# A graph attention layer on one core: the softmax sums one turn behind the scores, one-hots made first, four row buffers

## The chip, the cores and the metric

One Trainium2 chip, and of it one core: TensorE (PE), VectorE (DVE), ScalarE (ACT), GpSimd (POOL) and the queue engine SyncE (SP). The metric is the device time of one execution in microseconds; lower is better.

## The reference

There are 12,500 nodes with 128 features and 400,000 edges, sorted by target. Two blocks follow each other, each with a layer norm, a ReLU, a graph layer and a residual. The first graph layer is relational: two rounds that average rows by relation and multiply them with ten matrices. The second is graph attention (GAT), with four heads of 32 features, and the change lies in it:

```python
xl = (x @ W_l).reshape(n, H, C)
xr = (x @ W_r).reshape(n, H, C)
xj = xl[src]
xi = xr[dst]
e = jax.nn.leaky_relu(xi + xj, NEG_SLOPE)
score = jnp.einsum('ehc,hc->eh', e, att)
m = jax.ops.segment_max(score, dst, num_segments=n)
ex = jnp.exp(score - m[dst])
denom = jax.ops.segment_sum(ex, dst, num_segments=n)
alpha = ex / (denom[dst] + 1e-16)
out = jax.ops.segment_sum(alpha[..., None] * xj, dst, num_segments=n)
return out.reshape(n, H * C) + bias
```

A softmax over the edges of each target needs the largest score of a target before its exponentials, and a target's edges can lie across two groups of edges.

## The kernel before

The edges are cut into G = 125 groups of 128 x 25 edges: each of 128 partitions holds J = 25 consecutive edges of the sorted list. A first stage (up to about 450 us) makes tables, a second (to about 4400 us) and a third (to about 8340 us) do the two relational rounds, and the fourth, from about 8370 us to the end, does the attention. Each edge stage fetches a group's source rows by 25 indirect DMAs that GpSimd issues, one for each of the 25 edge columns (`gather`, L365; `gather_halves`, L382, in the stages before). A row in the attention stage has 132 numbers: `xl` and its four products with the attention vector.

In the attention stage the order of the instructions on each engine is the order in which they are written, since a manual schedule is in force (L893): a loop over turns `t` (L894), and in each turn steps that belong to different groups. In turn t:

- `gather` and `load` (L897, L898) for group t. `load` fetches by SP's queue the first target's number, the target rows `xr`, rows of targets `db` and the penalties `pen`.
- `prepare` (L932) for group t: VectorE makes `st` (L779) and `mk` (L782), ACT makes `pk`, and four matmuls make `xn` (L788), the target rows of each partition's first and last edges in its two halves.
- scores for group t-1, in four parts of 7, 6, 7 and 5 edge columns (`PARTS`). For each, ACT copies the first target's row into `z`, a PSUM tile (`first_xr`, L794), and VectorE replaces it where the target changes (L800), adds the gathered rows (L802), multiplies (L804) and reduces (L806). Two `z` copies for the first two parts stand at the turn's start, the others behind parts 0 and 1.
- `maxima` for group t-1: running maxima along each partition in both directions (scans, L760 and L763), transposed by TensorE and copied by ACT to `ro`.
- `inflow` for group t-3: two scans over the 128 partitions (`tr`, L830, and `br`, L835 and L839) carry maxima from one partition to the next. `tr` begins with the last value of the group before, copied by ACT (L829). `br` begins with eight partitions of the group after, so its `ro` must be there. TensorE transposes both and ACT copies them to `io` (L845).
- `less_maxima` for group t-3: L851 takes `io` in, scans spread the maxima, and they are subtracted from the scores (L857).
- `sums` for group t-3: five times for five columns, ACT makes exponentials (L862), VectorE weights the rows with them (`xw`, L863) and makes one-hots of the targets (`s`, L867), and TensorE adds up five matmuls (L871). `xw` and `s` have three buffers each. A last matmul (L874) takes in the group before.
- for group t-4: ACT copies the sums from PSUM to `su` (L906), and `finish` divides by the denominators (L880 to L883), adds the residual (L885) and stores the rows (L887). The last two groups go to a scratch table as well, and the last 128 rows of the output are copied from it at the end (L937).

Gathered rows have five buffers (`gx`, L731), and they are needed from turn t to turn t+3.

Of the kernel before, what the change touches and what calls it, by code (L numbers as in the profile page):

```python
# [9 lines left out]
F32 = mybir.dt.float32  # L10
# [3 lines left out]
OP = mybir.AluOpType  # L14
# [4 lines left out]
P = 128  # L19
J = 25  # L20
# [6 lines left out]
def kernel(  # L27
# [29 lines left out]
    nc = tc.nc  # L57
# [243 lines left out]
    def sorted_edges():  # L301
# [4 lines left out]
        with tc.tile_pool(name="sd", bufs=1, space=DRAM) as sd, tc.tile_pool(name="sk", bufs=1) as sk:  # L306
# [66 lines left out]
            with tc.tile_pool(name="mid", bufs=1) as mid:  # L373
# [58 lines left out]
                def sums(ps, s, rs, rows):  # L432

                    for k in range(2):
                        for c in range(2):
                            a, b = s[:, 2 * k + c, :], rs[k][:, c, :]
                            if not rows:
                                a, b = b, a
                            nc.tensor.matmul(ps, a, b, start=(k == 0 and c == 0), stop=(k == 1 and c == 1),  # L439
                                             skip_group_check=True)  # L440
# [287 lines left out]


            PARTS = [(j0 + a, min(JP, n - a), k) for k, (j0, n) in enumerate(HALVES) for a in range(0, n, JP)]  # L730
            with tc.tile_pool(name="gk", bufs=1) as kp, tc.tile_pool(name="gx", bufs=5) as xp, \  # L731
                    tc.tile_pool(name="gw", bufs=2) as wp, tc.tile_pool(name="gs", bufs=3) as sp, \
                    tc.tile_pool(name="gc", bufs=4) as cp, tc.tile_pool(name="gn", bufs=6) as np_, \
                    tc.tile_pool(name="gp", bufs=1, space=PSUM) as p1, \
                    tc.tile_pool(name="gp2", bufs=2, space=PSUM) as p2:
# [55 lines left out]
                def first_xr(xn, part):  # L791
                    j0, n, k = part
                    z = p2.tile([P, JP, D], F32, name="z")
                    nc.scalar.copy(z[:, :n, :], xn[:, 2 * k, None, :].to_broadcast([P, n, D]))  # L794
                    return z
# [30 lines left out]
                def inflow(g, ros, pens, before):  # L826

                    tr = wp.tile([H, P + 1], F32, name="tr")
                    nc.scalar.copy(tr[:, 0:1], before[:, P:] if g else lows)  # L829
                    nc.vector.tensor_tensor_scan(tr[:, 1:], pens[g][:, 0, :], ros[g][:, 0, :], tr[:, 0:1],  # L830
                                                 op0=OP.add, op1=OP.max)
                    br = wp.tile([H, P + 8], F32, name="br")
                    if g < G - 1:

                        nc.vector.tensor_tensor_scan(br[:, P + 7:P - 1:-1], pens[g + 1][:, 1, 7::-1],  # L835
                                                     ros[g + 1][:, 1, 7::-1], LOW, op0=OP.add, op1=OP.max)
                    else:
                        nc.scalar.copy(br[:, P:P + 1], lows)
                    nc.vector.tensor_tensor_scan(br[:, P - 1::-1], pens[g][:, 1, ::-1], ros[g][:, 1, ::-1],  # L839
                                                 br[:, P:P + 1], op0=OP.add, op1=OP.max)  # L840
                    pc = p1.tile([P, 2 * P], F32, name="px")[:, :2 * H].rearrange("p (k h) -> p k h", k=2)
                    nc.tensor.transpose(pc[:, 0, :], tr[:, :P], ident[:H, :H])
                    nc.tensor.transpose(pc[:, 1, :], br[:, 1:P + 1], ident[:H, :H])
                    io = wp.tile([P, 2, H], F32, name="io")
                    nc.scalar.copy(io, pc)  # L845
                    return io, tr

                def less_maxima(g, sc, sm, io, pk):

                    for k, (e, j) in enumerate(ends):  # L850
                        nc.vector.scalar_tensor_tensor(sm[:, :, j], io[:, k, :], e[:, g:g + 1], sm[:, :, j],  # L851
                                                       op0=OP.add, op1=OP.max)
                    up = wp.tile([P, H, J], F32, name="up")
                    scan_up(up, pk, sm)
                    mx = wp.tile([P, H, J], F32, name="dn")
                    scan_down(mx, pk, up)
                    nc.vector.tensor_sub(sc, sc, mx)  # L857

                def sums(g, xs, sc, po, before):
                    for j0 in range(0, J, JW):  # L860
                        xw = sp.tile([P, JW, H, AW], F32, name="xw")
                        nc.scalar.activation(xw[:, :, :, C], sc[:, :, j0:j0 + JW].rearrange("p h j -> p j h"), AF.Exp)  # L862
                        nc.vector.tensor_mul(  # L863
                            xw[:, :, :, :C], xs[:, j0:j0 + JW, :D].rearrange("p j (h c) -> p j h c", h=H),
                            xw[:, :, :, C:].to_broadcast([P, JW, H, C]))
                        s = sp.tile([P, JW, P], F32, name="s")
                        nc.vector.tensor_tensor(s, iotab[:, None, :].to_broadcast([P, JW, P]),  # L867
                                                dst_b[:, g, j0:j0 + JW, None].to_broadcast([P, JW, P]),
                                                op=OP.is_equal)
                        for j in range(JW):  # L870
                            nc.tensor.matmul(po, s[:, j, :], xw[:, j].rearrange("p h a -> p (h a)"),  # L871
                                             start=(j0 + j == 0), stop=(j0 + j == J - 1), skip_group_check=True)
                    if g:
                        nc.tensor.matmul(po[0:1, :], ecol[:, g - 1:g], before, start=False, stop=True,  # L874
                                         skip_group_check=True)
# [12 lines left out]
                    if g >= G - 2:  # L888
                        nc.sync.dma_start(o_d[ds(b, P), :], o)

                xs, xn, xr, dbs, bs, pens, scs, sms, ros, pks, x2s, pos, sums_of = ({} for _ in range(13))
                tr = None
                with tc.manual_schedule():  # L893
                    for t in range(G + 4):  # L894

                        if t < G:
                            xs[t] = gather(xp, xl_d[:N, :], src_i[:, t, :], XW)  # L897
                            xr[t], dbs[t], pens[t], bs[t] = load(t)  # L898
                        q = t - 3
                        if 0 <= q < G:  # L900
                            x2s[q] = cp.tile([P, D], F32, name="x2")
                            nc.sync.dma_start(x2s[q], x2_d[q])
                        q = t - 4
                        if 0 <= q < G:
                            sums_of[q] = cp.tile([P, H * AW], F32, name="su")
                            nc.scalar.copy(sums_of[q], pos.pop(q))  # L906
                        q = t - 1
                        if 0 <= q < G:
                            scs[q] = cp.tile([P, H, J], F32, name="sc")
                            zs = [first_xr(xn[q][0], p) for p in PARTS[:2]]  # L910
                        q = t - 3
                        if 0 <= q < G:
                            io, tr = inflow(q, ros, pens, tr)
                        q = t - 1
                        if 0 <= q < G:
                            for i, p in enumerate(PARTS[:2]):
                                scores(zs[i], xs[q], *xn[q][:2], scs[q], p)
                                zs.append(first_xr(xn[q][0], PARTS[2 + i]))
                        q = t - 4
                        if 0 <= q < G:  # L920
                            finish(q, sums_of[q], x2s.pop(q), bs.pop(q))
                        q = t - 3
                        if 0 <= q < G:
                            less_maxima(q, scs[q], sms.pop(q), io, pks.pop(q))
                        q = t - 1
                        if 0 <= q < G:
                            for i, p in enumerate(PARTS[2:]):
                                scores(zs[2 + i], xs[q], *xn[q][:2], scs[q], p)
                            pks[q] = xn.pop(q)[2]
                            sms[q], ros[q] = maxima(xs[q], scs[q], pks[q])  # L930
                        if t < G:
                            xn[t] = prepare(t, xr.pop(t), dbs.pop(t))  # L932
                        q = t - 3
                        if 0 <= q < G:
                            pos[q] = p1.tile([P, H * AW], F32, name="po")
                            sums(q, xs.pop(q), scs.pop(q), pos[q], sums_of.pop(q - 1, None))
                nc.sync.dma_start(out[N - P:N, :], o_d[N - P:N, :])  # L937


# [423 lines left out]
```

## Time and profile before

| | |
|---|---|
| median of 3 runs (range) | 12567.6 us (12566.2 to 12571.2) |
| the profiled execution, its span | 12565.0 us, 12563.2 us |
| first and last gather of the attention stage | 8370.8, 12479.3 us |
| busy from 8370.8 to the last gather's end at 12480.2 (4109.4 us) | DVE 3433.6, POOL 3157.4, PE 1322.0, ACT 655.7 us |
| from the last gather's end to the span's end | 83.0 us |
| a gather | 0.944 us at its shortest, 1.010 in the mean, 0.30 between two |
| L863 and L867 | 0.82 us each, five of each for a group |
| busy over the whole span | DVE 73%, POOL 73%, PE 26%, ACT 20% |

Times in views of the profile are in us from the span's start. A group of instructions is shown as line, engine, operation, tiles, count, then busy time and the mean ns of one, then the engine's idle time just before these instructions and what ended most of it. A row of the timeline has start, duration, engine, line, operation and tiles; idle time before it, if any, stands in brackets. "issue" means that nothing shown was waited for.

### The profile page before, as it was taken

To read this page: it belongs to the slowest core of one execution; us is meant where nothing else is said; L and a number is where in the kernel's file an instruction comes from. 1 tells how busy PE (TensorE), PEld (TensorE's weight loads), DVE (VectorE), ACT (ScalarE), POOL (GpSimd) and SP (SyncE) were. 2 spreads that over 40 slices of the span, in tenths; PEclk is the share of its full clock that TensorE was granted. 3 is DMA by queue.
4 is the path that set the end of the run, shared out by engine and by line. 5 is a ranking of instruction groups with operands and counts; after the bars stand their busy time and mean duration, and the time that the engine had idled before them with its cause. 6 is when DMAs were issued, how large, how long until landed. Compare 5 with 4: busy or idle time off the path is not lost.

```text
span 12563.2 us, 69544 instructions
## 1 busy us (share of the span) xinstructions
PE 3260.9 (26%) x12778; PEld 2155.0 (17%) x12778; DVE 9221.3 (73%) x12886; ACT 2511.7 (20%) x6895; POOL 9143.9 (73%) x9384
## 2 busy tenths in 40 slices
PE   7422222222222211111111111113333333333333
PEld 3111111111111100000000000012222222232323
DVE  5777777777777666666666666668888888888888
ACT  3333333333333300000000000001111111111111
POOL 0477777777777777777777777767777777777775
PEclk9655555555555555555555555556666666666666
DMA  6433333333333222222222222222222222222222
GB/s 211 139 94 95 96 96 96 96 95 94 97 96 96 86 62 61 61 61 61 61 61 61 61 61 61 61 59 62 62 61 62 62 63 61 62 61 63 61 63 47
DMA packets 608616, 964.64 MB, mean 77 GB/s; under 512 B 193888, under 2 KB 413610, under 8 KB 608170
## 3 DMA queue, kind: packets, MB, share of 16 engines
q0 software_dynamic: 300000, 621.40, 20.5%
q1 hardware_dynamic: 278906, 267.68, 6.6%
q10 hardware_dynamic: 29264, 71.04, 1.5%
q14 instruction: 340, 2.79, 0.1%
q8 instruction: 106, 1.74, 0.1%
HBM read 758.60 MB, written 200.85 MB: 76 GB/s over the span
## 4 chain that ended last, share of the span: by engine, by line
POOL 62%; issue 24%; DVE 5%; DMA 5%; PE 3%; ACT 1%; ACTq 0%; DVEq 0%; SPq 0%; POOLq 0%
POOL xs L382 43%; POOL xs L365 20%; DMA xs<-t_d,idx 3%; PE ps L288 2%; PE po L871 1%; DMA xs<-xl_d,src_i 1%; DVE z L802 1%; DVE z L800 1%; DVE lr L804 1%; DVE sc L806 1%; DMA xt<-in_x_dram 0%; ACT z L794 0%; DVE s L867 0%; PE pa L294 0%; DVE up L760 0%
## 5 line engine op out<-in xcount | busy, mean ns | idle before, releaser
L382 POOL DMA_INDIRECT xs<-t_d,idx x6250 | 5984.6, 958 | 1941.3 <-issue 1862.7
L365 POOL DMA_INDIRECT xs<-xl_d,src_i x3125 | 3157.4, 1010 | 984.4 <-issue 931.3
L402 DVE TENSOR_TENSOR y<-xs,wk 128x3072 f32<-128x3072 f32 (+1 forms) x375 | 1324.6, 3532 | 1229.5 <-DMA xs<-t_d,idx 1215.0
L405 DVE TENSOR_REDUCE r<-y 128x256 f32<-128x3072 f32 (+1 forms) x375 | 2102.2, 5606 | 30.5 <-DVE y L402 0.9
L414 ACT ACTIVATE y<-xs,wk 128x128 f32<-128x128 f32 x3000 | 1202.6, 500 | 639.6 <-DMA xs<-t_d,idx 616.8
L439 PE MATMUL ps<-r,s 128*128 128x128 f32 x1000 | 305.5, 461 | 3390.8 <-DVE r L405 3390.8
L592 PE MATMUL pt<-wall,hT 128*128 128x512 f32 x750 | 639.2, 989 | 1533.4 <-ACT ts L594 1533.4
L871 PE MATMUL po<-xw,s 128*128 128x132 f32 x6250 | 933.2, 317 | 70.0 <-DVE s L867 60.7
L871 PEld LDWEIGHTS po<-xw,s 128*128 128x128 f32 x6250 | 896.4, 228 | 118.9 <-issue 116.8
L439 PEld LDWEIGHTS ps<-r,s 128*128 128x128 f32 x1000 | 231.9, 322 | 3517.8 <-DVE r L405 3517.8
L121 ACT ACTIVATE sd<-mv,epsc 128x1 f32<-128x1 f32 x223 | 63.6, 293 | 3549.4 <-DVE mv L119 3524.4
L820 PE MATMUL px<-ident,up 128*4 128x128 f32 x125 | 46.5, 372 | 2398.1 <-DVE up L760 2398.1
L596 DVE TENSOR_TENSOR ts<-pt,xb 128x128 f32<-128x128 f32 x125 | 36.5, 292 | 851.5 <-ACT ts L594 851.5
L863 DVE TENSOR_TENSOR xw<-xs,xw 128x640 f32<-128x640 f32 x625 | 513.2, 821 | 91.2 <-ACT xw L862 85.8
L794 ACT COPY z<-xn 128x896 f32<-128x896 f32 x500 | 397.1, 813 | 757.8 <-DVE lr L804 743.9
L802 DVE TENSOR_TENSOR z<-xs,z 128x896 f32<-128x896 f32 x500 | 498.0, 996 | 46.1 <-DMA xs<-xl_d,src_i 29.3
L592 PEld LDWEIGHTS pt<-wall,hT 128*128 128x128 f32 x750 | 210.0, 320 | 1842.5 <-ACT ts L594 1713.2
L867 DVE TENSOR_TENSOR s<-iotab,dst_b 128x640 f32<-128x640 bf16 x625 | 511.2, 818 | 0.0
L804 DVE SCALAR_TENSOR_TENSOR lr<-z,att 128x896 f32<-128x896 f32 x500 | 495.5, 991 | 17.2
L806 DVE TENSOR_REDUCE sc<-lr 128x28 f32<-128x896 f32 x500 | 494.0, 988 | 17.1
L800 DVE COPY_PREDICATED z<-mk,xn 128x896 f32<-128x896 int32 x500 | 490.3, 981 | 7.1 <-ACT z L794 7.1
L439 PE MATMUL ps<-s,r 128*128 128x128 f32 x1000 | 305.1, 461 | 644.8 <-DVE r L420 644.8
(206 smaller groups left out, 6140.6 us busy)
## 6 DMA issues: line engine op xcount, KB each, us to landing
xs<-t_d,idx POOLq DMA_INDIRECT x6250, 2.5
t_d<-ts SPq DMA_DIRECT2D x125, 640.0 KB
m<-in_edge_attr_dram SPq DMA_DIRECT2D x125, 525.0 KB
t_d<-ts ACTq DMA_DIRECT2D x98, 640.0 KB
xs<-xl_d,src_i POOLq DMA_INDIRECT x3125, 2.6
db<-drow_d SPq DMA_DIRECT2D x125, 128.0 KB
xl_d<-ts SPq DMA_DIRECT2D x125, 66.0 KB
at<-accT_d SPq DMA_DIRECT2D x125, 64.0 KB
```

Source lines behind the costliest of these rows:

```text
L365: nc.gpsimd.indirect_dma_start(out=xs[:, j, :], out_offset=None, in_=table, in_offset=bass.IndirectOffsetOnAxis(ap=ids[:, j:j + 1], axis=0))
L382: nc.gpsimd.indirect_dma_start(out=x[:, j, :], out_offset=None, in_=table, in_offset=bass.IndirectOffsetOnAxis(ap=ids[:, j0 + j:j0 + j + 1 ...
L402: nc.vector.tensor_mul(y[:, :, :n, :], xs[:, None, :n, :].to_broadcast([P, 2, n, D]), wk[:, :, :n, None].to_broadcast([P, 2, n, D]))
L405: nc.vector.tensor_reduce(r, y[:, :, :n, :].rearrange("p c j d -> p c d j"), AX.X, OP.add)
L414: nc.scalar.activation(y[:, c, :, j], xs[:, j, :], AF.Copy, scale=wk[:, c, j:j + 1])
L439: nc.tensor.matmul(ps, a, b, start=(k == 0 and c == 0), stop=(k == 1 and c == 1), skip_group_check=True)
L592: nc.tensor.matmul(pt[:, :n], hT, wall[:, c:c + n], start=True, stop=True)
L800: nc.vector.copy_predicated(z, mk[:, j0:j0 + n, None].to_broadcast([P, n, D]), xn[:, 2 * k + 1, None, :].to_broadcast([P, n, D]))
L802: nc.vector.tensor_add(z, xs[:, j0:j0 + n, :D], z)
L804: nc.vector.scalar_tensor_tensor(lr[:, :n, :], z, 0.0, att8[:, None, :].to_broadcast([P, n, D]), op0=OP.max, op1=OP.mult)
L806: nc.vector.tensor_reduce(sc[:, :, j0:j0 + n].rearrange("p h j -> p j h"), lr[:, :n, :].rearrange("p j (h c) -> p j h c", h=H), AX.X, OP.add)
L871: nc.tensor.matmul(po, s[:, j, :], xw[:, j].rearrange("p h a -> p (h a)"), start=(j0 + j == 0), stop=(j0 + j == J - 1), skip_group_check=True)
```

## The change

The loop has G + 1 turns in place of G + 4. In turn t the scores and maxima are those of group t-1 as before, but `inflow`, `less_maxima` and `sums` are those of group t-2 and stand at the end of the turn, behind `prepare`. So `br` of group t-2 uses the `ro` that the same turn's `maxima` have just made. One-hots become a function of their own, with six buffers: two are made before `inflow`, three between it and `less_maxima`, and the five `xw` follow each other. The sums of group t-3 are copied to `su` behind part 1 of the scores, and `finish` for it stands behind part 2. In the last turn (t = G) groups G-2 and G-1 both go through sums and finish. Gathered rows are needed from turn t to turn t+2 and have four buffers.

```diff
-            with tc.tile_pool(name="gk", bufs=1) as kp, tc.tile_pool(name="gx", bufs=5) as xp, \
+            with tc.tile_pool(name="gk", bufs=1) as kp, tc.tile_pool(name="gx", bufs=4) as xp, \
                     tc.tile_pool(name="gw", bufs=2) as wp, tc.tile_pool(name="gs", bufs=3) as sp, \
+                    tc.tile_pool(name="go", bufs=6) as op, \
...
-                def sums(g, xs, sc, po, before):
+                def one_hots(g, j0):
+                    s = op.tile([P, JW, P], F32, name="s")
+                    nc.vector.tensor_tensor(s, iotab[:, None, :].to_broadcast([P, JW, P]),
+                                            dst_b[:, g, j0:j0 + JW, None].to_broadcast([P, JW, P]),
+                                            op=OP.is_equal)
+                    return s
+
+                def sums(g, xs, sc, ss, po, before):
...
-                        s = sp.tile([P, JW, P], F32, name="s")
-                        nc.vector.tensor_tensor(s, iotab[:, None, :].to_broadcast([P, JW, P]),
-                                                dst_b[:, g, j0:j0 + JW, None].to_broadcast([P, JW, P]),
-                                                op=OP.is_equal)
                         for j in range(JW):
-                            nc.tensor.matmul(po, s[:, j, :], xw[:, j].rearrange("p h a -> p (h a)"),
+                            nc.tensor.matmul(po, ss[j0 // JW][:, j, :], xw[:, j].rearrange("p h a -> p (h a)"),
...
-                    for t in range(G + 4):
+                    for t in range(G + 1):
 
                         if t < G:
                             xs[t] = gather(xp, xl_d[:N, :], src_i[:, t, :], XW)
                             xr[t], dbs[t], pens[t], bs[t] = load(t)
-                        q = t - 3
-                        if 0 <= q < G:
-                            x2s[q] = cp.tile([P, D], F32, name="x2")
-                            nc.sync.dma_start(x2s[q], x2_d[q])
...
+                        for q in ([t - 2] if t < G else [G - 2, G - 1]):
+                            if q >= 0:
+                                x2s[q] = cp.tile([P, D], F32, name="x2")
+                                nc.sync.dma_start(x2s[q], x2_d[q])
                         q = t - 1
-                        if 0 <= q < G:
+                        if q >= 0:
                             scs[q] = cp.tile([P, H, J], F32, name="sc")
                             zs = [first_xr(xn[q][0], p) for p in PARTS[:2]]
...
+                            for i, p in enumerate(PARTS):
                                 scores(zs[i], xs[q], *xn[q][:2], scs[q], p)
...
+                                if i < 2:
+                                    zs.append(first_xr(xn[q][0], PARTS[2 + i]))
+                                if i == 1 and q >= 2:
+                                    take(q - 2)
+                                if i == 2 and q >= 2:
+                                    end(q - 2)
                             pks[q] = xn.pop(q)[2]
                             sms[q], ros[q] = maxima(xs[q], scs[q], pks[q])
                         if t < G:
                             xn[t] = prepare(t, xr.pop(t), dbs.pop(t))
...
+                        for q in ([t - 2] if t < G else [G - 2, G - 1]):
+                            if q >= 0:
+                                ss = [one_hots(q, j0) for j0 in (0, JW)]
+                                io, trs[q] = inflow(q, ros, pens, trs.pop(q - 1))
+                                ss += [one_hots(q, j0) for j0 in range(2 * JW, J, JW)]
+                                less_maxima(q, scs[q], sms.pop(q), io, pks.pop(q))
+                                pos[q] = p1.tile([P, H * AW], F32, name="po")
+                                sums(q, xs.pop(q), scs.pop(q), ss, pos[q], sums_of.pop(q - 1))
+                                if t == G:
+                                    take(q)
+                                    end(q)
```

`take(q)` is the copy to `su`, and `end(q)` calls `finish`.

More of the change, by code (lines that the diff above doesn't have):

```diff
@@ L889, in finish, with take, end @@
                         nc.sync.dma_start(o_d[ds(b, P), :], o)
-                xs, xn, xr, dbs, bs, pens, scs, sms, ros, pks, x2s, pos, sums_of = ({} for _ in range(13))
-                tr = None
+                xs, xn, xr, dbs, bs, pens, scs, sms, ros, pks, x2s, pos, trs = ({} for _ in range(13))
+                sums_of = {-1: None}
+                def take(q):
+                    sums_of[q] = cp.tile([P, H * AW], F32, name="su")
+                    nc.scalar.copy(sums_of[q], pos.pop(q))
+                def end(q):
+                    finish(q, sums_of[q], x2s.pop(q), bs.pop(q))
+                trs[-1] = None
                 with tc.manual_schedule():
-                    for t in range(G + 4):
+                    for t in range(G + 1):
                         if t < G:
@@ L898, in sorted_edges @@
                             xr[t], dbs[t], pens[t], bs[t] = load(t)
-                        q = t - 3
-                        if 0 <= q < G:
-                            x2s[q] = cp.tile([P, D], F32, name="x2")
-                            nc.sync.dma_start(x2s[q], x2_d[q])
-                        q = t - 4
-                        if 0 <= q < G:
-                            sums_of[q] = cp.tile([P, H * AW], F32, name="su")
-                            nc.scalar.copy(sums_of[q], pos.pop(q))
+                        for q in ([t - 2] if t < G else [G - 2, G - 1]):
+                            if q >= 0:
+                                x2s[q] = cp.tile([P, D], F32, name="x2")
+                                nc.sync.dma_start(x2s[q], x2_d[q])
@@ L907, in sorted_edges @@
                         q = t - 1
-                        if 0 <= q < G:
+                        if q >= 0:
                             scs[q] = cp.tile([P, H, J], F32, name="sc")
                             zs = [first_xr(xn[q][0], p) for p in PARTS[:2]]
[L911 to L916, printed above, removed]
-                                scores(zs[i], xs[q], *xn[q][:2], scs[q], p)
-                                zs.append(first_xr(xn[q][0], PARTS[2 + i]))
@@ L919, in sorted_edges @@
[L919 to L928, printed above, removed]
+                            for i, p in enumerate(PARTS):
+                                scores(zs[i], xs[q], *xn[q][:2], scs[q], p)
+                                if i < 2:
[4 more added lines that the diff above has]
+                                    end(q - 2)
@@ L932, in sorted_edges @@
                             xn[t] = prepare(t, xr.pop(t), dbs.pop(t))
[L933 to L936, printed above, removed]
+                        for q in ([t - 2] if t < G else [G - 2, G - 1]):
[9 more added lines that the diff above has]
+                                    end(q)
                 nc.sync.dma_start(out[N - P:N, :], o_d[N - P:N, :])
```

## The prediction

> **What bounds the kernel now.** The change touches the last of the three edge stages, so I read the stretch after 8450 us alone, first as groups of instructions (busy us, mean ns, idle before and who ended it).
>
> ```profile
> L365 POOL DMA_INDIRECT xs<-xl_d,src_i x3062 | 3098.0, 1012 | 933.1 <-issue 912.4 <-DMA xs<-xl_d,src_i 7.6 <-DVE up L760 2.1
> ...
> L863 DVE TENSOR_TENSOR xw<-xs,xw 128x640 f32<-128x640 f32 x625 | 513.2, 821 | 91.2 <-ACT xw L862 85.8
> L867 DVE TENSOR_TENSOR s<-iotab,dst_b 128x640 f32<-128x640 bf16 x625 | 511.2, 818 | 0.0
> L802 DVE TENSOR_TENSOR z<-xs,z 128x768 f32<-128x768 f32 x491 | 488.9, 996 | 24.3 <-DMA xs<-xl_d,src_i 7.5
> ...
> L830 DVE TENSOR_TENSOR_SCAN tr<-pen,tr,ro 4x128 f32<-4x128 f32 x124 | 58.7, 473 | 463.7 <-ACT tr L829 463.7
> ...
> L906 ACT COPY su<-po 128x132 f32<-128x132 f32 x125 | 33.5, 268 | 463.6 <-PE po L874 460.5 <-PE po L871 3.1
> ```
>
> The gathers (L365) never wait for a buffer: their idle time is the same 0.30 us ahead of each. VectorE hardly waits for rows (L802), but 463.7/124 = 3.7 us a turn for the carried maximum `tr`. ACT hands that over behind `su`, which waits for the last matmul of the previous group's sums, and behind two 0.8 us copies. Two engines are thus nearly full; the timeline tells which one sets the pace. First and last of 118 turns (start, duration):
>
> ```profile
> 8585.07 1.10 DVE L802 TENSOR_TENSOR z<-xs,z 128x896 f32<-128x896 f32 x1
> 8595.52 0.94 POOL L365 DMA_INDIRECT xs<-xl_d,src_i  x1 [0.30 <-issue]
> ...
> 12479.25 0.94 POOL L365 DMA_INDIRECT xs<-xl_d,src_i  x1 [0.30 <-issue]
> 12498.73 1.10 DVE L802 TENSOR_TENSOR z<-xs,z 128x896 f32<-128x896 f32 x1
> ```
>
> The first row addition of group 6 starts 10.45 us before that group's last gather, that of group 124 19.48 us after it. VectorE's turn is (12498.73-8585.07)/118 = 33.17 us, the gathers' period (12479.25-8595.52)/118 = 32.91. VectorE is the bound by only 0.26 us a turn. Taking its wait away can therefore win little unless the gathers also get faster, so the next question is what a gather period is made of. Early on, without sums, it is 31.2 us (8370.77 to 8401.98: 25 x 0.944 + 25 x 0.304). The other 1.7 us are gathers that VectorE holds up:
>
> ```profile
> 10362.18 0.95 POOL L365 DMA_INDIRECT xs<-xl_d,src_i  x1 [0.30 <-issue]
> 10363.43 1.56 POOL L365 DMA_INDIRECT xs<-xl_d,src_i  x1 [0.30 <-issue]
> 10365.30 1.17 POOL L365 DMA_INDIRECT xs<-xl_d,src_i  x1 [0.30 <-issue]
> ...
> 10363.36 0.82 DVE L867 TENSOR_TENSOR s<-iotab,dst_b 128x640 f32<-128x640 bf16 x1
> 10364.09 0.82 DVE L863 TENSOR_TENSOR xw<-xs,xw 128x640 f32<-128x640 f32 x1
> 10364.83 0.82 DVE L867 TENSOR_TENSOR s<-iotab,dst_b 128x640 f32<-128x640 bf16 x1
> ```
>
> The gather at 10363.43 falls into the one-hot that ends at 10364.18 and itself ends 0.82 us later, though `xw` is running by then. Over the whole stage one rule fits: an access 0.125 us after a gather's start waits if it falls into a running L863, L867, scan, L779 or L883, from about 0.15 us after that operation's start to its end (0.07 before it for scans); then 0.82 us remain. Operations with an input in PSUM (L802, L804; L402 in layer 2) never delay one. So a turn's ten back-to-back L863/L867, 0.735 us apart, cost one entry (0.62) and four times 0.22 (two such operations against a 1.25 us gather) = 1.5 us; scans, L779 and L883 the other 0.2.
>
> **The Trainium skill against this row.** "SBUF — State Buffer", section "Who interferes with whom", says that a VectorE instruction with two SBUF inputs contends with a GpSimd instruction that reads SBUF, that the lock is held for the whole instruction, and that the loser fully blocks. The trace agrees on which operations block (z and layer 2's weights are in PSUM). Counted with the rule alone, each of ten 0.82 us operations met at random costs 0.82^2/2/1.25 = 0.27 us, 2.7 a turn, a period of 34.1 us and a slower kernel. The row says less: 0.67 us is the blocked part, and a waiting gather gets in between two operations. I take the row.
>
> **The change, part by part.**
> *VectorE's turn.* Its instructions are the same. Start to start in the timeline, one turn holds four parts of scores 4.35 + 3.85 + 4.38 + 3.44, finish 0.94, maxima 0.91, prepare 0.74, inflow scans 1.0, less_maxima 1.37, ten L863/L867 7.35: 28.3 us. Before, 3.77 (tr), 0.73 (exp) and small gaps make it 33.2.
> - The wait for `tr` goes: the scan now needs `ro`, which ACT has 0.9 us after the maxima (10029.85 to 10030.72), while prepare and two one-hots run for 2.2 us. `su` is copied amid the scores, 8 us after the sums.
> - L851 waits for two transposes and a copy, 0.26 + 0.24 + 0.17 plus handovers, some 0.9 us; three one-hots (2.2 us) cover it. Without that cover it is 0.9 a turn. On TensorE the transposes now stand ahead of the 25 sum matmuls and behind four `xn` matmuls, which end 2.0 us after `st`; `tr` is ready later than that. Behind `io` on ACT are the exponentials, which need L851 anyway.
> - New: five L863 without one-hots between run into TensorE. `xw` has three buffers, so the fourth exponential waits for the first five matmuls: ten passes at 0.215 us (the pace of `xn`, idle engine) or 0.113 (later in the sums), that is 1.1 to 2.2 us. Worked along the row, the fourth L863 loses 1.5 and the fifth 0.6 when cold, about 0.5 in all when warm. I take cold, since TensorE rests 4 us before. With exp's 0.45 and 0.1 for the next `z` copy: 28.3 + 2.1 + 0.55 = 31.0 us. So VectorE falls below the gathers' 31.2 and waits for them.
>
> *The gathers' period* now decides: 31.2 plus what VectorE blocks. Blocking time is the same, but in groups of two and three one-hots, three L863 close together and two apart. And VectorE, waiting for the last gather's rows, now starts at a fixed distance from it: 1.65 to 1.83 us, as in the first three groups. I laid the turn out from the last gather's end. Accesses of the next group come at 0.43, 1.68, ..., 5.42 us. With VectorE starting at 1.80, st blocks from 5.50, just too late for the fifth; those that follow lose 0.10, 0.17, 0.06 and 0.22, that is 0.55. With 1.65, st catches the fifth (0.18), and then 0.50, 0.46, 0.22, 0.06, 0.22 and a later 0.18 follow: 1.8. Arrivals at random give 0.35 for the pair, 0.48 for each trio, 0.36 for the two single L863 and 0.2 for the rest: 1.9. The landing scatters by more than the 0.1 us that separates the cases, so both should occur; I take the middle, 1.2, hence 32.4 us, with ends 31.7 and 33.1.
>
> *The end.* Before, 83.0 us pass from the last gather (12480.19) to the end. After: landing 1.8, rest of the last part 2.6, maxima 0.9; then twice one-hots 3.7, scans 1.0, less_maxima 1.4, exp and L863 5.8, matmuls to `su` 2.2, finish 0.7 = 14.8; then 7.7 for the two output DMAs as now (12555.5 to 12563.2). Sum 42.6; with the handovers in it 44. This saves 39 us.
>
> *The rest.* Four row buffers with rows kept one turn less: a gather waits for sums that end two gather periods earlier, less 18, so 46 us ahead; free. If that cover went, a gather would wait for VectorE's turn end. SP: x2 loads and output stores move up a turn behind the same five loads; SP waits for `o` as before, and its loads are for a group whose rows take 32 us to come; free. One-hots have six buffers for five a turn; free.
>
> *Sum.* Gathers start at 8370.8; the first three groups run at 31.2 (93.6). Span = 8370.8 + 93.6 + 122 x 32.4 + 44 = 12461. The profiled execution lies 1.8 above its span (12565.0 against 12563.2) and 2.6 below the median, so 12466 us. Before, the same sum breaks even at a period of 33.24, 2.04 us of blocking.
>
> **The rivals.**
> - *Lucky phase:* the gathers slip past st every turn, 31.75 us: 12387. For it: two of the first three groups start at 1.83. Against: scatter. It can't go below VectorE's 31.0.
> - *Blocking like random arrivals*, 33.05: 12545, where the only gain is the end. For it: nothing in the trace has one-hots back to back, and the present 1.7 is itself a locked rhythm.
> - *Slower:* a gather isn't let in between two like operations. Seen is only s to xw, xw to s and scan to scan. A pair would then hold it for 1.4 - 0.62 = 0.8 us, a trio for 2.14 - 0.62 = 1.5: 0.8 + 1.5 + 1.5 + 0.36 + 0.2 = 4.4, period 35.6, about 12855. It decides from 2.04 us of blocking on. Against it: the gap of 0.065 us between the blocked parts of overlapping operations is where gathers get in now, and it should be the same for two of a kind.
> - *The wait moves instead of going:* VectorE stays the bound because TensorE stays slow in all 25 matmuls or L851 does wait. At most 28.3 + 0.55 + 2.6 + 0.9 = 32.4, still no slower than the forecast's gathers: about 12470.
>
> **How the numbers follow.** Forecast (or the moved wait, which gives the same time) 0.45, lucky phase 0.26, random-like 0.20, slower 0.09. A measurement of this kernel tells about 0.2% (25 us). Faster by over 0.2% means below 12542: forecast, lucky and nearly half of random-like, 0.82; within it, the rest of that, 0.10; slower 0.08, with a sliver of its rival only breaking even. The range leaves out a sliver of lucky, some random-like and the slower rival: 12380 to 12560. The likeliest case alone: 12420 to 12510.
>
> **What the profile after would show.** Right: `tr` without idle time before it; L802 waiting for rows in every turn, its start 1.7 us after a last gather; fourth and fifth L863 waiting for exponentials; L365 mean 944 + 1200/25 = 990 ns; some 45 us from last gather to end. Wrong: L365 above 1025 ns with durations near 2 us, which is the slower rival; or gathers waiting for DVE; or L802 not waiting for rows, VectorE's turn then being over 32 us for a wait I have not seen.

## The result and the profile after

The changed kernel takes 12664.2 us in the median of four runs (12656.4 to 12675.1), the kernel before 12568.3 us beside it (12566.2 to 12571.2). The ratio is 1.0076, with a 95% interval of 1.0061 to 1.0091: it is slower by 0.8%, where 12466 us had been forecast. On some chips the kernel before takes 14360 to 14440 us instead of 12570; ratios measured there are marked "other pace" below.

The profiled executions, 12656.4 against 12565.0 us, split this difference (all in us):

| | before | after | forecast for after |
|---|---|---|---|
| first gather of the attention stage | 8370.8 | 8371.1 | 8370.8 |
| from there to the last gather's end | 4109.4 | 4237.0 | 4046.4 |
| from the last gather's end to the span's end | 83.0 | 46.5 | 44 |
| a turn, from VectorE's row additions | 33.17 | 33.93 | 32.4 |
| a gather, in the mean | 1.010 | 1.051 | 0.990 |
| added to a turn's gathers by VectorE | 1.72 | 2.74 | 1.2 |

The end became shorter by 36.5 us, nearly as forecast. The stretch of the gathers became longer by 127.6 us. The difference of the two, with a start that is 0.3 us later, is the 91.4 us by which the execution is slower. "Added" is the sum, over a turn's 25 gathers, of what each takes beyond the 0.943 us of an undelayed one, in the mean of the last 122 groups. It grew by 1.02 us a turn. Over all 3125 gathers the growth is 127.5 us: all of it.

The groups of instructions of the changed kernel, from 8450 to 12620 us (busy us and mean ns, then idle time before them and who ended it):

```profile
L365 POOL DMA_INDIRECT xs<-xl_d,src_i x3065 | 3225.1, 1052 | 934.1 <-issue 917.6 <-DVE o L889 8.5 <-DVE o L887 6.1
...
L803 DVE TENSOR_TENSOR z<-xs,z 128x896 f32<-128x896 f32 x492 | 489.9, 996 | 223.0 <-DMA xs<-xl_d,src_i 185.7 <-issue 21.5 <-DVE z L801 5.6
...
L871 DVE TENSOR_TENSOR xw<-xs,xw 128x640 f32<-128x640 f32 x613 | 484.3, 823 | 364.2 <-ACT xw L870 364.2
L862 DVE TENSOR_TENSOR s<-iotab,dst_b 128x640 f32<-128x640 bf16 x615 | 468.4, 806 | 0.0
...
L831 DVE TENSOR_TENSOR_SCAN tr<-pen,tr,ro 4x128 f32<-4x128 f32 x123 | 57.5, 468 | 0.0
...
L852 DVE SCALAR_TENSOR_TENSOR sm<-io,ends,sm 128x4 f32<-128x4 f32 x246 | 42.3, 208 | 0.0
```

The carried maximum (L831), which had cost 463.7 us of idle time before, now costs none, and L852 none either. VectorE instead waits for rows (L803, 185.7 us behind a gather's landing), so the gathers do set the pace now. But one gather has a mean of 1052 ns, where 990 was expected. The timeline of one turn shows where that goes (start, duration; idle time in brackets):

```profile
10503.41 1.55 DVE L862 TENSOR_TENSOR s<-iotab,dst_b 128x640 f32<-128x640 bf16 x2
...
10504.33 1.44 POOL L365 DMA_INDIRECT xs<-xl_d,src_i  x1 [0.30 <-issue]
...
10505.84 2.26 DVE L862 TENSOR_TENSOR s<-iotab,dst_b 128x640 f32<-128x640 bf16 x3
...
10506.08 2.85 POOL L365 DMA_INDIRECT xs<-xl_d,src_i  x1 [0.30 <-issue]
...
10509.23 0.95 POOL L365 DMA_INDIRECT xs<-xl_d,src_i  x1 [0.31 <-issue]
...
10509.89 2.29 DVE L871 TENSOR_TENSOR xw<-xs,xw 128x640 f32<-128x640 f32 x3 [0.37 <-ACT xw L870]
10510.48 1.05 POOL L365 DMA_INDIRECT xs<-xl_d,src_i  x1 [0.30 <-issue]
...
10513.65 0.83 DVE L871 TENSOR_TENSOR xw<-xs,xw 128x640 f32<-128x640 f32 x1 [1.47 <-ACT xw L870]
...
10515.69 0.82 DVE L871 TENSOR_TENSOR xw<-xs,xw 128x640 f32<-128x640 f32 x1 [1.22 <-ACT xw L870]
```

The gather of 10506.08 reaches for SBUF 0.125 us after its start, in the first of three one-hots. That one-hot ends near 10506.63, but the gather ends only at 10508.93. Take off the 0.82 us that remain once it is let in, and it was let in at 10508.11: at the end of the third one-hot (10505.84 + 2.26 = 10508.10). The gather of 10510.48 falls into the first of three `xw`, just as closely packed, and is let in by the same count at 10510.71. That is the end of the first `xw`, while the second is running. This gather came late, 0.72 us after the start of that `xw`, as nearly all of the 123 that met the first `xw` of a turn did, and so late one-hot 1 lets gathers in too (below); whether `xw` differ from one-hots is decided by a later run with five `xw` in a row.

Over the whole stage, each gather was set against the one-hot in which its access falls (the earlier one where two overlap), and the moment it was let in against the ends of the one-hots:

| access falls in one-hot | 1 | 2 | 3 | 4 | 5 |
|---|---|---|---|---|---|
| gathers, all of them delayed | 85 | 38 | 80 | 43 | 0 |
| delay, us a turn | 0.33 | 0.15 | 1.23 | 0.49 | 0.00 |

One-hots 1 and 2 are the pair ahead of `inflow`, 3 to 5 the trio behind it. Of the 246 gathers, 81 were let in at the first end of a one-hot that came, 85 at the second and 80 at the third. Of the 81, 38 fell into one-hot 2, behind which a scan stands; the other 43 came in the last hundredths of one-hot 1, 0.72 to 0.74 us after its start, when the next was about to start or had just started. The one-hots add 2.21 us a turn in all, the five `xw` 0.45.

### The profile page after: what moved, and what is told of

Read it like the earlier page. It is cut to its first block, busy times and chain, and to the rows that moved or that the text cites. A ratio compares the mean times of both kernels' runs of the same rounds, so it can differ in the third digit from the quotient of the medians.

```text
span 12654.6 us, 68801 instructions
## 1 busy us (share of the span) xinstructions
PE 3349.1 (26%) x12778; PEld 2251.9 (18%) x12778; DVE 9215.0 (73%) x12886; ACT 2513.3 (20%) x6895; POOL 9269.7 (73%) x9384
## 4 chain that ended last, share of the span: by engine, by line
POOL 64%; issue 24%; DMA 5%; DVE 4%; PE 3%; ACT 1%; ACTq 0%; SPq 0%; POOLq 0%; DVEq 0%
POOL xs L382 42%; POOL xs L365 22%; DMA xs<-t_d,idx 4%; PE ps L288 2%; DMA xs<-xl_d,src_i 1%; DVE z L803 1%; DVE lr L805 1%; PE po L875 1%; DVE sc L807 0%; DVE z L801 0%; DVE s L862 0%; ACT z L795 0%; DMA xt<-in_x_dram 0%; PE pa L294 0%; DMA dst_i<-in_dst_dram 0%
## 5 line engine op out<-in xcount | busy, mean ns | idle before, releaser
L365 POOL DMA_INDIRECT xs<-xl_d,src_i x3125 | 3284.9, 1051 | 984.5 <-issue 935.6
L875 PE MATMUL po<-xw,s 128*128 128x132 f32 x6250 | 1010.4, 339 | 567.3 <-DVE xw L871 567.3
L875 PEld LDWEIGHTS po<-xw,s 128*128 128x128 f32 x6250 | 986.0, 250 | 578.2 <-DVE xw L871 573.5
L803 DVE TENSOR_TENSOR z<-xs,z 128x896 f32<-128x896 f32 x500 | 497.9, 996 | 244.7 <-DMA xs<-xl_d,src_i 207.4
L862 DVE TENSOR_TENSOR s<-iotab,dst_b 128x640 f32<-128x640 bf16 x625 | 476.0, 806 | 0.0
```

The source lines that it names most:

```text
L365: nc.gpsimd.indirect_dma_start(out=xs[:, j, :], out_offset=None, in_=table, in_offset=bass.IndirectOffsetOnAxis(ap=ids[:, j:j + 1], axis=0))
L803: nc.vector.tensor_add(z, xs[:, j0:j0 + n, :D], z)
L875: nc.tensor.matmul(po, ss[j0 // JW][:, j, :], xw[:, j].rearrange("p h a -> p (h a)"), start=(j0 + j == 0), stop=(j0 + j == J - 1), skip_gr ...
```

## The experiments

Two theories were tried. *No hand-over:* one-hots that follow each other keep a gather out until the last of them ends, and this alone makes the kernel slower. *Other waits:* the new waits of `xw` for TensorE (1.47 and 1.22 us in the rows above), or some other effect of the new order, make it slower. What is asked of each run is therefore its time and, in its trace, which gathers are delayed by what.

Ratios of the other pace tell nothing about the gathers' pace. In those traces VectorE waits longer for the other engines and the gathers wait 2.4 to 8.2 us a turn for row buffers, so only their records of which gather is delayed by which operation are used. The changed kernel with the row of numbers in PSUM has a trace of each kind: `xw` lasts 824 ns on the chip of the usual pace and 822 on the other, a one-hot 803 and 804, but VectorE's wait before `xw` is 3.0 and 5.6 us a turn. Why is not known.

### The one-hots' row of numbers in PSUM

The one-hot compares two inputs, both in SBUF: 128 numbers in a row, and the targets. This run puts the row into PSUM and leaves the order of the changed kernel as it is.

```diff
+                iotap = p1.tile([P, P], F32, name="iotap")
+                nc.vector.tensor_copy(iotap, iota)
...
-                    nc.vector.tensor_tensor(s, iotab[:, None, :].to_broadcast([P, JW, P]),
+                    nc.vector.tensor_tensor(s, iotap[:, None, :].to_broadcast([P, JW, P]),
```

The first three of these runs are of the other pace, the last is of the usual one.

> The changed kernel, with the row of node numbers that the one-hots compare with held in PSUM, so that a one-hot has one SBUF input. Theory A (two or three one-hots back to back keep a gather out until the last of them ends, 2.2 us of the 2.76 us that VectorE holds up per turn): the 2.2 us go, 0.55 stay, the gathers could do 31.8 us a period; VectorE's own turn, 32.0 by the trace of the changed kernel, becomes the bound: mean period 32.1 in place of 33.95, about 12440 us. Theory B (the one-hots are not the cause; the gathers lose time to the scans and the place of the turn): 12650 to 12670 us, L365 mean stays at 1050 ns.

> The changed kernel with the row of node numbers in PSUM, once more, now beside the next three. Theory A: VectorE's turn of 32.0 us, with its waits for TensorE, is the bound: about 12440 us, ratio 0.990. Theory B: 12650 to 12670 us, ratio 1.007.

> The changed kernel with only the row of node numbers in PSUM, where the kernel before takes about 12570 us. Theory A: gathers lose 0.6 to 0.9 us a turn, so they could do 32.0 us; VectorE, with its 3.7 us of waits for TensorE and ACT in a turn, has 32.0 as well: period 32.1 to 32.4, 12440 to 12480 us, ratio 0.990 to 0.993; little behind the run with five xw buffers. Theory B: ratio 1.007.

> As e1c_iota_psum. Where the kernel before takes about 12570 us: theory A 12440 to 12480 us, ratio 0.990 to 0.993; theory B ratio 1.007. Where it takes over 14300 us: 0.991 again.

Measured on a chip of the usual pace: 12512.2 us, ratio 0.9951 (0.9934 to 0.9967). Other pace: 0.9909 (0.9892 to 0.9926), 0.9906 (0.989 to 0.9923) and 0.9918 (0.9902 to 0.9935). In the trace of the 12512 us run, 296 gathers reach for SBUF while a one-hot runs, and none of them is delayed; added time falls from 2.74 to 1.40 us a turn. The groups, from 8450 to 12380 us:

```profile
L365 POOL DMA_INDIRECT xs<-xl_d,src_i x3015 | 3011.2, 999 | 919.3 <-issue 887.6 <-DMA xs<-xl_d,src_i 14.6 <-DVE rd L887 7.6
...
L805 DVE TENSOR_TENSOR z<-xs,z 128x896 f32<-128x896 f32 x482 | 479.7, 995 | 49.2 <-DMA xs<-xl_d,src_i 29.4 <-DVE z L803 3.3
...
L873 DVE TENSOR_TENSOR xw<-xs,xw 128x640 f32<-128x640 f32 x602 | 476.2, 824 | 363.3 <-ACT xw L872 363.3
...
L864 DVE TENSOR_TENSOR s<-iotap,dst_b 128x640 f32<-128x640 f32 x605 | 459.0, 803 | 0.0
```

The one-hot itself is as fast as before (803 ns against 806). The waits of `xw` are still there (363 us, 3.0 a turn), and yet the kernel is faster than both: so one-hots that keep gathers out are what made the changed kernel slower, not these waits. The size was missed: 12440 to 12480 us had been forecast. The `xw` now delay gathers by 1.13 us a turn rather than 0.45, since gathers that no one-hot holds up arrive elsewhere; and VectorE hardly waits for rows any more (49 us against 223), so that its own turn, with the waits of `xw` in it, lies close under the gathers' 32.6 us. Its first gather also came 22 us later (8392.6) than in the kernel before, in stages that the edit doesn't touch. A run of another edit on the same chip, the one below with each one-hot behind its `xw`, has it 20 us later too (8390.4), so this is not the edit's doing.

### The same row in the kernel before

```diff
-                        nc.vector.tensor_tensor(s, iotab[:, None, :].to_broadcast([P, JW, P]),
+                        nc.vector.tensor_tensor(s, iotap[:, None, :].to_broadcast([P, JW, P]),
```

> The kernel before, with the same PSUM row and nothing else. If VectorE's turn of 33.17 us was the bound before, as read from the trace, the gathers drop to about 31.6 us and then wait for row buffers, and the time stays: 12555 to 12575 us. If the gathers set the pace before, it falls by 1.2 us a turn, to about 12420 us.

> The kernel before with the row of node numbers in PSUM, once more, beside the others. If VectorE's 33.17 us is the bound before: ratio 0.998 to 1.0. If the gathers set the pace before: ratio 0.988.

> The kernel before with the row of node numbers in PSUM, where it takes about 12570 us. If VectorE's turn of 33.17 us was the bound, gathers now lose 0.7 us in place of 1.7, run ahead until row buffers hold them, and the time stays: ratio 0.998 to 1.0. If the gathers set the pace: 1.0 us a turn less, ratio 0.990.

> The kernel before with the row in PSUM, on a chip that runs the kernel before near 12570 us. If VectorE sets the pace before (turn 33.17 us against 32.91 of the gathers), freeing the gathers from the one-hots gives nothing: 12540 to 12590 us, ratio 0.998 to 1.001, with the gathers 0.8 us a turn faster where nothing else holds them, and waiting for row buffers instead. If the gathers set the pace before, their period falls from 32.9 to 32.1 us: 12470 us, ratio 0.992.

Measured: 0.999 (0.9981 to 0.9999), 0.9989 (0.9982 to 0.9996), 0.9994 (0.9986 to 1.0003) and 0.9988 (0.9981 to 0.9995), all four at the other pace. There the gathers of the last run have a mean of 969 ns and wait for row buffers instead, and the time stays. That is what a kernel bound by VectorE does; but on these chips VectorE waits for ACT, so it doesn't show that the same holds at the usual pace. Neither time expected there can be judged. That the row of numbers alone is worth little without the new order thus stays likely, and was not shown.

### What lets a gather in between two one-hots

Two runs ask why `xw` and `xw`, or `xw` and one-hot, let a gather in between, and two one-hots don't. One puts a short VectorE instruction ahead of one-hots 2, 4 and 5; the other takes both inputs in f32, as `xw` has them, in place of bf16.

```diff
+                    if j0 not in (0, 2 * JW):
+                        nc.vector.memset(gap, 0.0)
```

```diff
-                    nc.vector.tensor_tensor(s, iotab[:, None, :].to_broadcast([P, JW, P]),
-                                            dst_b[:, g, j0:j0 + JW, None].to_broadcast([P, JW, P]),
+                    nc.vector.tensor_tensor(s, iota[:, None, :].to_broadcast([P, JW, P]),
+                                            dst_f[:, g, j0:j0 + JW, None].to_broadcast([P, JW, P]),
```

> The changed kernel with a VectorE memset of 128x8 between two one-hots of a pair or trio (three a turn). If a gather gets in as soon as one-hots don't follow each other directly, each one-hot blocks for itself, as in the kernel before: about 1.0 us for the five in place of 2.2, a period of 32.8, about 12525 us, and no L365 over 1.8 us. If the short operation doesn't let it in: 12660 to 12690 us.

> The changed kernel with one-hots made from the float32 copies of both inputs in place of the bf16 ones, both still in SBUF. If it is the bf16 inputs that keep the gather out between two one-hots (L871 with float32 inputs lets it in between two of its kind): about 12525 us, with no L365 over 1.8 us. If it is not the type: 12650 to 12670 us, with L365 up to 2.9 us.

Measured, both at the other pace: 0.9953 (0.9937 to 0.997) with the instruction between, 0.9843 (0.9826 to 0.9859) with f32. From the timeline with the instruction between:

```profile
11000.97 1.56 DVE L865 TENSOR_TENSOR s<-iotab,dst_b 128x640 f32<-128x640 bf16 x2
11001.46 1.14 POOL L365 DMA_INDIRECT xs<-xl_d,src_i  x1 [0.30 <-issue]
11001.74 0.07 DVE L864 MEMSET gap<- 128x8 f32 x1
...
11004.15 2.36 POOL L365 DMA_INDIRECT xs<-xl_d,src_i  x1 [0.30 <-issue]
...
11004.89 0.80 DVE L865 TENSOR_TENSOR s<-iotab,dst_b 128x640 f32<-128x640 bf16 x1
```

The gather of 11001.46 is let in at 11001.78 (its end less 0.82), where the first one-hot of the pair ends. The gather of 11004.15 is let in at 11005.69, the end of the last one-hot of the trio (11004.89 + 0.80), past a `memset`. In the pair all 90 gathers that fell into its first one-hot were let in at that one-hot's end. Of the 121 that fell into the first two of the trio, 110 waited to the end of the third, and the other 11 got in at the end of the second only where the third began late. So the `memset` helps in one place and not in the other. In the trace it starts only 0.01 to 0.02 us after the next one-hot has started, 0.05 us before the one ahead ends, so the trace doesn't show it parting the two. The one-hots still add 1.77 us a turn. With f32:

```profile
11019.69 1.55 DVE L862 TENSOR_TENSOR s<-iota,dst_f 128x640 f32<-128x640 f32 x2
11020.18 1.88 POOL L365 DMA_INDIRECT xs<-xl_d,src_i  x1 [0.30 <-issue]
11022.12 2.26 DVE L862 TENSOR_TENSOR s<-iota,dst_f 128x640 f32<-128x640 f32 x3
11022.36 2.84 POOL L365 DMA_INDIRECT xs<-xl_d,src_i  x1 [0.30 <-issue]
```

Both gathers wait to the end of the last one-hot, at 11021.24 and 11024.38; the one-hots add 2.36 us a turn, and all 121 gathers that fell into the first two of a trio waited to its end. The type is not the reason. The lower time of this run says nothing on the gathers, which are slower in it (mean 1069 ns) than in the changed kernel.

### Each one-hot behind its weighted rows again

All else of the change stays (one turn behind, the last two groups in one turn, four row buffers); only the order of one-hots and `xw` is that of the kernel before. No one-hots then stand between `inflow` and `less_maxima`.

```diff
-                def sums(g, xs, sc, ss, po, before):
+                def sums(g, xs, sc, po, before):
...
+                        s = one_hots(g, j0)
...
-                                ss = [one_hots(q, j0) for j0 in (0, JW)]
                                 io, trs[q] = inflow(q, ros, pens, trs.pop(q - 1))
-                                ss += [one_hots(q, j0) for j0 in range(2 * JW, J, JW)]
```

> The changed kernel with each one-hot again behind its xw, as in the kernel before, and inflow and less_maxima one after the other without one-hots between; all else as changed. Theory A (back to back is the cause): L365 falls to the blocking of the kernel before, 1.7 us a turn, so 32.9 us a period, while VectorE has about 30.5: span 8434 + 122 x 32.9 + 46 = 12494, about 12500 us, ratio 0.995. Theory B (the place of the turn behind the gather's landing, not the order of one-hots, makes the gathers lose time): about 12650 us.

> The changed kernel with each one-hot behind its xw again. Theory A: no gather waits past the end of one operation; blocking is that of ten alternating operations, 1.5 to 1.9 us a turn, period 32.7 to 33.1, so 12475 to 12525 us, ratio 0.993 to 0.996. Theory B (place of the turn behind the landing): 12650 us, ratio 1.007.

> The changed kernel with each one-hot behind its xw again, where the kernel before takes about 12570 us. Theory A: no gather waits past the end of one operation, 1.1 to 1.9 us a turn are lost (1.1 and 1.2 in the earlier two runs of it), period 32.3 to 33.1, so 12430 to 12525 us, ratio 0.989 to 0.996. Theory B: 12650 us, ratio 1.007.

> As e6c_onehots_between. Where the kernel before takes about 12570 us: theory A 12430 to 12525 us, ratio 0.989 to 0.996; theory B 12650 us, ratio 1.007. Where it takes over 14300 us, VectorE's waits for a standing ACT set the pace and the ratio says nothing of the gathers: 0.997 again.

Measured at the usual pace: 12511.6 us, ratio 0.995 (0.9934 to 0.9967). Other pace: 0.9974 (0.9963 to 0.9985), 0.9976 (0.9969 to 0.9983) and 0.9977 (0.9969 to 0.9984). The groups of the 12512 us run, from 8450 to 12380 us:

```profile
L365 POOL DMA_INDIRECT xs<-xl_d,src_i x3012 | 3013.8, 1001 | 918.2 <-issue 901.4 <-DMA xs<-xl_d,src_i 12.8 <-DVE o L890 3.7
...
L803 DVE TENSOR_TENSOR z<-xs,z 128x640 f32<-128x640 f32 x481 | 478.7, 995 | 224.6 <-DMA xs<-xl_d,src_i 183.5 <-issue 22.6 <-DVE z L801 7.1
...
L831 DVE TENSOR_TENSOR_SCAN tr<-pen,tr,ro 4x128 f32<-4x128 f32 x121 | 57.3, 474 | 48.1 <-ACT tr L830 44.6 <-ACT pk L786 2.0 <-issue 1.5
...
L852 DVE SCALAR_TENSOR_TENSOR sm<-io,ends,sm 128x4 f32<-128x4 f32 x242 | 43.8, 223 | 101.4 <-ACT io L846 101.4
```

From its timeline:

```profile
10520.86 0.81 DVE L862 TENSOR_TENSOR s<-iotab,dst_b 128x640 f32<-128x640 bf16 x1
10521.34 1.16 POOL L365 DMA_INDIRECT xs<-xl_d,src_i  x1 [0.30 <-issue]
10521.60 0.81 DVE L871 TENSOR_TENSOR xw<-xs,xw 128x640 f32<-128x640 f32 x1
```

Here the row of numbers is still in SBUF and 401 gathers of the stage are delayed by a one-hot, but each only to that one-hot's end, as the one in these rows (10521.34 + 1.16 - 0.82 = 10521.68, where the one-hot ends and `xw` already runs). None takes longer than 1.60 us, where 126 of the changed kernel took more than 2. The added time is 1.44 us a turn, the turn 32.64 us. The waits that the one-hots had covered are back, 101.4/121 = 0.84 us at L852 and 0.4 at L831, and they cost nothing, because VectorE still waits 224.6 us for rows. So the one-hots made ahead covered waits that nothing on the path felt, and their packing was paid by the gathers. Of the whole change, this part alone turns a gain of 0.5% into a loss of 0.8%.

### Five buffers for the weighted rows

With five buffers in place of three, no `xw` waits for the matmuls of its own group.

```diff
-                    tc.tile_pool(name="go", bufs=6) as op, \
+                    tc.tile_pool(name="go", bufs=6) as op, tc.tile_pool(name="gv", bufs=5) as vp, \
...
-                        xw = sp.tile([P, JW, H, AW], F32, name="xw")
+                        xw = vp.tile([P, JW, H, AW], F32, name="xw")
```

> The changed kernel with the row of node numbers in PSUM and five xw buffers in place of three, so that no exponential waits for TensorE. Theory A (one-hots back to back keep gathers out, and with them gone VectorE's waits for TensorE are next): gathers 31.8 us a period, VectorE's turn about 29.5, span 8434 + 122 x 31.8 + 46 = 12360, about 12365 us, ratio 0.984. Theory B (blocking by one-hots is not what made the change slower): no faster than the changed kernel, ratio 1.005 to 1.01.

> The same as e5_iota_psum_xw5 (row of node numbers in PSUM, five xw buffers), once more. Where the kernel before takes about 12568 us, theory A gives 12365 us, ratio 0.984; theory B 1.005 to 1.01. On the chip of e5, where the kernel before takes 14365 us and ACT stands still for some 10 us in each turn for a reason outside this change, it will be 1.02 again.

> The changed kernel with five buffers for weighted rows and no other edit. If the one-hots in a row are what costs the time, the time stays: 12640 to 12700 us, ratio 1.006 to 1.011, blocked time 2.8 to 3.1 us a turn, since VectorE was waiting for the gathers anyway. If the waits of the fourth and fifth weighted rows were what slowed the turn (1.5 and 1.2 us), it falls to about 12330 us, ratio 0.981.

The edit is shown against the changed kernel; the first two runs add the row in PSUM to it.

Measured, row in PSUM and five buffers: at the usual pace 12438.5 us, ratio 0.989 (0.9873 to 0.9906); at the other pace 1.0234 (1.0217 to 1.0251), which stays unexplained. Five buffers alone: 1.001 (1.0003 to 1.0017), at the other pace only, so neither of the two times expected of it can be judged; in its trace, the one-hots add 2.16 us a turn, nearly the 2.21 of the changed kernel, so the waits of `xw` have no part in that. The timeline of the 12438 us run, one-hots and `xw`:

```profile
10406.62 1.55 DVE L864 TENSOR_TENSOR s<-iotap,dst_b 128x640 f32<-128x640 f32 x2
10407.55 0.94 POOL L365 DMA_INDIRECT xs<-xl_d,src_i  x1 [0.30 <-issue]
...
10409.05 2.25 DVE L864 TENSOR_TENSOR s<-iotap,dst_b 128x640 f32<-128x640 f32 x3
10410.18 0.94 POOL L365 DMA_INDIRECT xs<-xl_d,src_i  x1 [0.30 <-issue]
...
10413.08 3.77 DVE L873 TENSOR_TENSOR xw<-xs,xw 128x640 f32<-128x640 f32 x5 [0.37 <-ACT xw L872]
10413.92 1.54 POOL L365 DMA_INDIRECT xs<-xl_d,src_i  x1 [0.30 <-issue]
10415.77 1.17 POOL L365 DMA_INDIRECT xs<-xl_d,src_i  x1 [0.30 <-issue]
```

Gathers begin amid two and three one-hots and take the 0.94 us that is their shortest; of 339 such in the whole stage none is delayed. Among five `xw` in a row they are delayed and let in at the next end (10413.92 + 1.54 - 0.82 = 10414.64, the end of the second). All 246 gathers that met one of the first four `xw` got in so, having come 0.18 to 0.61 us after its start; in the changed kernel no gather that came so early in a one-hot got in before the one-hot that follows directly. The groups, from 8450 to 12380 us:

```profile
L365 POOL DMA_INDIRECT xs<-xl_d,src_i x3062 | 2998.1, 979 | 933.1 <-issue 911.5 <-DMA xs<-xl_d,src_i 14.0 <-DVE o L891 6.7
...
L805 DVE TENSOR_TENSOR z<-xs,z 128x896 f32<-128x896 f32 x489 | 487.1, 996 | 431.4 <-DMA xs<-xl_d,src_i 371.1 <-issue 49.4 <-DVE z L803 2.5
...
L873 DVE TENSOR_TENSOR xw<-xs,xw 128x640 f32<-128x640 f32 x615 | 463.3, 820 | 45.1 <-ACT xw L872 45.1
```

The added time is 0.90 us a turn, the turn 32.10 us, and VectorE waits 431/122 = 3.5 us a turn for rows: the gathers, with 31.2 us of their own and 0.9 added, now bound the stage. The expected span of 12360 us was missed by 78: that sum counts 124 groups instead of 125 (31.8 us), the period is 0.3 us longer (37 us in 122 turns; `xw` alone add 0.77 us a turn), and the first gather came 10 us later (8381.0). This version is faster than both kernels, by 1.1% against the one before.

## Why the prediction was wrong

- *VectorE's turn.* Right in what counts: it fell below the gathers' pace, the wait for `tr` went, as did any wait at L852, and the last part of the scores now waits for rows in every one of the last 122 groups, starting 1.8 us after the last gather in the median. Its size was missed by a little: the waits that replaced it are 0.37, 1.47, 1.22 and 0.68 us (first, fourth and fifth `xw`, next `z` copy) against 0.45, 1.5, 0.6 and 0.1, so that the turn without waits for rows is 33.93 - 223/123 = 32.1 us instead of 31.0. The fifth `xw` waits longer because the second five matmuls are nearly as slow as the first (its exponential starts 2.0 us after the one before it). At 33.93 us a turn this costs nothing; at the 32.4 forecast it would have been near the bound.
- *The gathers' period.* Here is the step that failed: "Blocking time is the same, but in groups of two and three one-hots", together with what was taken from the trace of before, "a waiting gather gets in between two operations". Seen there were one-hot to `xw` (380 of 380) and `xw` to one-hot (145 of 145), never two one-hots; it was carried over to them by argument. It holds for two `xw` (246 of 246 in the run with five in a row), not for one-hots. The pair adds 0.49 us, the trio 1.72, the `xw` 0.45 and all else 0.1: 2.74 us in place of 1.2. (The 990 ns given for the mean gather are 992 by the prediction's own sum, 944 + 1200/25.)
- *The rule weighed against the row.* The rule of the Trainium skill ("SBUF — State Buffer", section "Who interferes with whom", and for the whole instruction its section "SBUF: two separate sides") says that the one that starts first holds the shared ports for the whole instruction and the other waits. Worked alone it gave a period of 34.1 us; measured are 33.93. The two are near each other by another way than the rule's: a single operation does block only 0.67 us, as the row said, but two or three one-hots block like one long one. What "Who interferes with whom" states of instructions with at most one input in SBUF is borne out by the runs with the row in PSUM, 635 accesses without a delay.
- *The rival.* "A gather isn't let in between two like operations" was the mechanism, with the point from which it decides (2.04 us of blocking) about right: 2.74 us make the kernel slower, and the sign named for it, L365 above 1025 ns with durations over 2 us, came. It was given 0.09, since "the gap of 0.065 us between the blocked parts" should be the same for any two operations; it isn't. Its price for the one-hots, 0.8 + 1.5 us, was nearly the 2.21 measured. In all it was too high (4.4 us, 12855 us), because it was applied to `xw` too, which do let gathers in: 0.45 us instead of 1.9.
- *The end.* 44 us forecast, 46.5 measured. Each of the last two groups took 16.7 to 16.9 us in place of 14.8: exponentials and `xw` 6.7 to 7.0 instead of 5.8, from the waits above, and the matmuls to `su` 2.9 instead of 2.2.
- *The sum.* 122 turns of 1.53 us more (186 us), 3 us at the end and 4 us in the first turns make the 194 us by which the span of 12654.6 exceeds the 12461 forecast.

That one-hots in a row made the kernel slower is shown twice: by putting one input in PSUM with the order kept, and by changing the order with the inputs kept. Why two one-hots don't let a gather in between and two `xw` do is open. They follow each other at the same distance (0.735 and 0.736 us). The type of the input is ruled out by the run with f32. Waits are not the reason either: one-hots 4 and 5 wait for TensorE's use of their buffers, one-hot 2 doesn't, and neither lets a gather in. Left untried are the operation itself (a comparison, where `xw` multiplies), the shape of the inputs (the one-hot repeats both of its inputs along a dimension, `xw` only one) and the output (the one-hot fills its tile, `xw` leaves every 33rd number out).

## What to carry to other kernels

When two engines are nearly even, ask what an edit to one does to the other's instructions, not only to its waits: here a gather issued by GpSimd became slower by up to 1.9 us each time it met VectorE instructions whose two inputs are both in SBUF, and the longest delays, beyond 0.66 us, came only because one-hots were moved next to each other. An interaction read from a trace holds for the pairs of instructions that are seen in it; for a new neighbourhood, take the worst case into the range. One input in PSUM, at no cost in the instruction's own time, took the one-hots' part in it away altogether.

## What was not expected of the hardware

- Two or three one-hots in a row (two SBUF inputs each) delayed a gather to the end of the last, unless it came 0.72 us or more into the first of the pair: up to 2.85 us instead of 0.94, while five `xw` in a row let it in at every end (246 of 246). A `memset` between them helped in the pair (90 of 90) and not in the trio.
- With one of the two inputs in PSUM, the same comparison took 803 ns as against 806, and delayed none of the 635 gathers that fell into it in two runs.
